# A convolution and LoRA layer on one core: gate mixing in eight tiles of the matmul array, conv weights by halves, and a new order of the first 620 steps

## The chip, the core and the metric

The kernel runs on one core of one Trainium2 chip. The metric is the device time of one execution in microseconds (us); the time shown is the median of several. A core has five engines that work side by side: TensorE (PE in the profile; PEld is its loading of weights), VectorE (DVE), ScalarE (ACT), GpSimd (POOL) and SyncE (SP), which here only issues DMAs. ACT issues DMAs too.

## The reference

The input `x` has shape (64, 64, 1024). A grouped 1-D convolution (4 groups, 9 taps) with a conditional bias goes in front of a linear layer with two LoRA terms; the result is added to `x`:

```python
out = lax.conv_general_dilated(x, weight, ..., feature_group_count=4)
y = out + einsum('nd,od->no', c, c_weight)[:, :, None] + bias[None, :, None]
...
base_out = matmul(y, kernel) + bias
A_eff = einsum('bn,nri->bri', gate, lora_A)
B_eff = einsum('bn,nor->bor', gate, lora_B)
delta = einsum('bor,btr->bto', B_eff, einsum('bri,bti->btr', A_eff, y))
delta = delta + einsum('or,btr->bto', lora_B_shared, einsum('ri,bti->btr', lora_A_shared, y))
x = x + base_out + delta
```

There are 8 gates of 16 entries; gate b mixes the 16 LoRAs for 8 samples. The shared LoRA is one for all.

## The kernel before

**Tiling.** The 64 samples are worked on as 16 pairs `p` of 4 samples each. For each pair and each of the four groups `g` the input is loaded (`xload`, 258 KB), split into a rounded high part and a rest (`xhi` on ACT, `xlo` on VectorE or GpSimd), and convolved by matmuls against a Toeplitz form of the weights, which is split in the same way (`th`, `tl`); three products high x high, low x high and high x low give the precision. Pairs 0 to 2 convolve directly (`conv`, 6 matmuls, line 318), later ones by a scheme with three half-size products, whose middle one (`convo`) uses the sum of the two weight blocks, and whose outer ones (`convd`) use differences of the input (`xdiff`, `xdhi`, `xdlo`, `xohi`, `xolo`; line 346). `evac` brings a convolution from PSUM to SBUF with its bias, `turned` transposes it on VectorE (line 387).

**The linear layer.** Pair 0 is multiplied plainly (`plain`, 3 matmuls, line 580), the other pairs by a Strassen-Winograd scheme of seven products on blocks of 512 x 512 (`prod`, 12 matmuls each, line 592), with block sums of the activations (`asum` on GpSimd) and of the weights (`wsum`), and splits `yhi`/`ylo` and `whi`/`wlo`. The weight pieces are loaded (`wload`), the shared LoRA's product is made by 16 matmuls (`fmm`, line 475, from `saload`, `sbload` and their splits) and added to them (`fadd`, line 479, VectorE). `keep`, `xsum`, `ysum`, `radd`, `yadd`, `total` combine the products with the residual (`rload`), and `store` writes 256 KB.

**The gated LoRA.** `lload w i` loads 16 tiles `ls` of 256 KB. `gload` and `gmask` build `gm`, the gates on a diagonal mask (lines 506 to 513). `mix w j` (line 528) multiplies: two float32 products of K 128, M 64, N 512 into the two halves of one PSUM tile. `mixout` (line 534, ACT) copies it over an `ls` tile, `mixput` (line 542) writes it in two DMAs of 128 KB to a DRAM tensor `eff`, and `aload` (line 550) and `bload` (line 556) read a gate's part back: 128 KB for A, three times 64 KB for each half of B. `lora p` (line 602) is 16 products of M 32 in four column tiles; `axlow`, `axsum`, `axhi`, `axlo` split its result, and `delta` (line 660) adds it to the accumulators.

**PSUM.** Five buffers of one bank each serve `fmm`, `mix`, `plain`, `prod` and the conditional bias (`cmul`), two serve the convolutions, one serves `lora`. A new user waits for the evacuation of an old one: `fmm` for a `fadd`, a convolution for its `evac` or `evmid`.

**Order.** One list, ORDER, of 1848 steps is written out in the code. Each step issues its instructions on its engines in this order, and no engine reorders. The last letter of a step chooses the engine: v VectorE, p GpSimd, a ACT. `xload`, `wload`, `lload`, `rload`, `mixput`, `aload`, `bload` issue on SP; `small`, `cwload`, `gload`, `ctload`, `store` on ACT. All DMAs share eight completion slots: each waits until the eighth before it has landed.

The start of the list, with `busy` (warming matmuls, line 701), `twload`, `thi`, `tlo`, `twsum` (weights of the convolution), and `cwide`, `cmul`, `csum` (conditional bias):

```python
small 1, warm, twload 1, busy 29, twload 0, cwload, gload, ctload, cwide, cmul, thi 2, small 0, thi 0, tlo 0 v,
xload 0 0, xhi 0 0, tlo 2 p, xload 0 1, xlo 0 0 v, conv 0 0, twsum v, xhi 0 1, xlo 0 1 v, conv 0 1, sbload 1,
```

Of the kernel before, what the change touches and what calls it, by code (L numbers as in the profile page):

```python
# [10 lines left out]
ALU = mybir.AluOpType  # L11
# [39 lines left out]
small 1, warm, twload 1, busy 29, twload 0, cwload, gload, ctload, cwide, cmul, thi 2, small 0, thi 0, tlo 0 v,  # L51
xload 0 0, xhi 0 0, tlo 2 p, xload 0 1, xlo 0 0 v, conv 0 0, twsum v, xhi 0 1, xlo 0 1 v, conv 0 1, sbload 1,
sbhi 1, csum, evac 0 0 v, turned 0 0, xload 0 2, xhi 0 2, xload 0 3, saload 0, sblo 1 p, xlo 0 2 p, evac 0 1 v,
turned 0 1, saload 1, gmask, xhi 0 3, conv 0 2, xlo 0 3 p, sahi 1, conv 0 3, sahi 0, salo 0 v, fmm 0 1,
sbload 0, sbhi 0, fmm 1 1, wload 1 0, evac 0 2 a, xload 1 0, sblo 0 v, fmm 1 0, salo 1 v, xload 1 1, xhi 1 0,
xhi 1 1, xlo 1 1 p, xlo 1 0 v, turned 0 2, yhi 0 0, ylo 0 0 p, wload 0 1, fadd 0 1, evac 0 3 a, fadd 1 0,
conv 1 0, whi 7 0, fmm 4 0, turned 0 3, xload 1 2, xhi 1 2, wlo 7 0 v, fmm 3 0, wload 1 1, conv 1 1, fadd 1 1,
wload 4 0, fmm 0 0, whi 0 1, wload 0 0, fadd 0 0, evac 1 0 a, plain 0 1 0, fadd 4 0, xlo 1 2 p, turned 1 0,
whi 0 0, wlo 0 1 p, fmm 2 1, fmm 2 0, yhi 0 7, evac 1 1 a, conv 1 2, fmm 5 0, wload 2 1, wload 2 0, fadd 2 0,
wlo 0 0 p, plain 0 0 0, xload 1 3, fadd 2 1, wload 5 0, xhi 1 3, fmm 4 1, xlo 1 3 p, plain 0 0 1, whi 0 2,  # L60
ylo 0 7 v, fadd 5 0, plain 0 3 0, whi 7 1, yhi 0 4, wload 3 0, fadd 3 0, whi 0 3, wload 5 1, fmm 3 1, conv 1 3,
turned 1 1, wlo 7 1 v, wload 3 1, xload 2 0, plain 0 1 1, fadd 3 1, whi 7 2, evac 1 2 v, wlo 7 2 p, wload 4 1,
wlo 0 3 p, wlo 0 2 v, lload 0 6, plain 0 2 0, whi 7 3, plain 0 3 1, fadd 4 1, wload 7 1, turned 1 2, whi 1 1,
plain 0 1 2, lload 0 7, xhi 2 0, plain 0 0 2, ylo 0 4 v, plain 0 3 2, xlo 2 0 v, plain 0 2 1, fmm 5 1,
evac 1 3 a, xload 3 0, wlo 7 3 v, plain 0 2 2, turned 1 3, whi 1 0, yhi 0 1, ylo 0 1 v, fadd 5 1, whi 6 1,
conv 2 0, wload 7 0, thi 1, xdiff 3 0 0 v, wload 6 0, evac 2 0 a, lload 1 5, wlo 1 0 p, fmm 7 0, fadd 7 0,
plain 0 2 3, plain 0 0 3, fmm 6 0, lload 0 2, plain 0 3 3, plain 0 1 3, fadd 6 0, lload 0 5, whi 6 0, asum 1 2,
yhi 1 2, lload 0 0, yhi 1 0, plain 0 0 4, plain 0 2 4, wsum 2 2 v, whi 2 2, lload 1 1, wlo 1 1 p, plain 0 0 5,
fmm 6 1, tlo 1 v, plain 0 2 5, rload 0 2, wlo 6 0 v, wsum 2 1 v, wsum 2 3 v, whi 1 2, wlo 1 2 v, plain 0 1 4,
whi 2 1, asum 1 3, whi 1 3, wlo 1 3 p, xload 2 2, wload 6 1, fadd 6 1, xload 2 1, whi 6 2, lload 0 1, xhi 2 2,  # L70
plain 0 3 4, lload 0 4, plain 0 2 6, lload 1 0, lload 0 3, wsum 2 0 v, fmm 7 1, plain 0 2 7, xload 2 3,
plain 0 0 6, fadd 7 1, whi 6 3, total 0 2, lload 1 6, mix 0 0, mixout 0 0 a, wlo 6 2 v, xhi 2 1, wlo 6 3 v,
wlo 6 1 v, wsum 3 2 v, xlo 2 2 v, mix 0 3, mixout 0 3 a, mix 0 2, mixout 0 2 a, wsum 3 0 v, wsum 5 0 v,
mixput 0 0, whi 2 3, mix 0 1, wsum 3 1 v, mix 1 0, mixput 0 3, mixout 0 1 a, xdiff 3 0 1 p, wsum 4 0 v,
conv 2 2, wlo 2 2 v, whi 2 0, wlo 2 0 v, ylo 1 2 v, plain 0 1 5, wsum 5 1 v, rload 0 0, wsum 5 2 v, wsum 4 2 v,
xlo 2 1 v, plain 0 0 7, mixput 0 1, ylo 1 0 p, mixput 0 2, wlo 2 1 v, prod 1 0, plain 0 1 6, wsum 3 3 v,
wsum 5 3 v, rload 0 1, plain 0 3 5, wsum 4 3 v, bihi, whi 3 2, keep 1 0, plain 0 1 7, lload 1 3, wsum 4 1 v,
plain 0 3 6, mixout 1 0 a, lload 1 7, mix 1 3, aload 0, whi 5 3, yhi 1 3, rload 0 3, lload 1 2, ylo 1 3 v,
mixout 1 3 a, total 0 1, lora 0, mix 1 1, turned 2 0, lora 1, whi 5 0, bilo, xohi 3 0, lload 1 4, mix 1 2,
whi 4 2, wlo 4 2 v, mixout 1 1 a, xolo 3 0 v, whi 3 0, wlo 3 0 v, wlo 3 2 v, yhi 1 1, ylo 1 1 v, mixout 1 2 a,  # L80
asum 1 5, total 0 0, whi 4 1, conv 2 1, axlow 1, axsum 1, xload 3 2, wlo 4 1 p, wlo 2 3 v, whi 4 0,
plain 0 3 7, axlow 0, axsum 0, mixput 1 0, mixput 1 3, wlo 4 0 v, xhi 2 3, xlo 2 3 v, wlo 5 3 v, axhi 1,
prod 1 1, biput 0, axlo 1, whi 3 3, asum 1 6, yhi 1 6, wlo 3 3 v, mixput 1 1, evac 2 1 a, turned 2 1, aload 1,
mixput 1 2, total 0 3, evac 2 2 v, turned 2 2, bload 0 0, whi 3 1, axhi 0, prod 1 2, keep 1 2, conv 2 3,
bhi 0 0, biput 1, yhi 2 0, evac 2 3 a, blo 0 0 v, axlo 0, yhi 1 4, bload 0 1, wlo 3 1 p, prod 1 3, ylo 2 0 v,
delta 0 0 1, total 0 0 1, bhi 0 1, blo 0 1 v, ylo 1 6 p, prod 1 6, whi 4 3, delta 0 3 1, wlo 4 3 v, store 0 0,
# [12 lines left out]
yadd 1 v, blo 1 0 v, xdhi 4 0, axlo 2, delta 2 0, yhi 2 6, evac 3 3, keep 2 2, xdlo 4 0 v, convo 4 0,
turned 3 3, convd 4 0, rload 2 0, evmid 4 0 a, total 1 3, total 2 0, ylo 3 0 v, lora 3, xdiff 4 1 0 v,  # L100
xdiff 4 1 1 p, asum 3 3, yhi 3 3, prod 3 0, convo 4 1, ylo 3 3 v, evac 4 0, turned 4 0, xdhi 4 1, xload 4 3,
xohi 4 3, xdlo 4 1 v, asum 3 2, xolo 4 3 v, yhi 3 2, ylo 2 6 v, xload 4 2, xdiff 4 2 0 p, store 1 2,
xdiff 4 2 1 p, xohi 4 2, prod 3 3, yhi 3 1, bload 1 1, evmid 4 1 a, delta 2 2, ylo 3 2 v, xolo 4 2 v, asum 3 5,
store 2 0, convd 4 1, xdhi 4 2, xsum 2, convo 4 2, evmid 4 2 a, evac 4 1, xdlo 4 2 v, rload 2 2, radd 2 2 p,
total 2 2, xdiff 4 3 0 v, xdiff 4 3 1 p, prod 2 6, turned 4 1, yhi 3 4, bhi 1 1, convd 4 2, evac 4 2, keep 3 0,
prod 3 2, ylo 3 1 v, rload 2 3, radd 2 3 v, ysum 2 v, convo 4 3, yadd 2 v, xdhi 4 3, xdlo 4 3 v, ylo 3 4 v,
aload 2, prod 3 1, convd 4 3, turned 4 2, blo 1 1 p, xload 5 0, yhi 3 5, xohi 5 0, keep 3 2, asum 3 6,
keep 3 3, xload 5 1, xohi 5 1, delta 2 3, prod 3 4, delta 2 1, xdiff 5 0 0 p, xdiff 5 0 1 v, axlow 3,
ylo 3 5 p, evmid 4 3 a, total 2 3, prod 3 5, store 2 3, xolo 5 0 p, rload 2 1, yhi 3 6, radd 2 1 p, rload 3 0,
axsum 3, evac 4 3, axhi 3, turned 4 3, yhi 4 0, axlo 3, delta 3 0, xload 5 2, xdhi 5 0, store 1 3, xdlo 5 0 v,  # L110
# [707 lines left out]
```

## Time and profile before

| what | value |
|---|---|
| median of 3 runs | 447.79 us (447.44 to 451.44) |
| the profiled execution's own time | 447.48 us |
| its span in the profile | 445.7 us |
| TensorE busy | 438.3 us, 98% |
| VectorE busy | 391.3 us, 88% |
| ACT busy | 251.2 us, 56% |
| GpSimd busy | 234.5 us, 53% |
| DMA | 67.05 MB, mean 150 GB/s |

Times in the profile count from the span's start. Busy time is the union of an engine's instructions; ends of matmuls are modelled, so one matmul's record overlaps the next one's, and what a matmul really takes is read from one start to the next. A row of a group has the line of the code, the engine, the operation, the tiles (out<-in), the count, and after the bar the busy time, the mean length in ns and the idle time before.

### The profile page before, as it was taken

The numbers are of one execution on the slowest core, as the hardware profiler recorded it, in microseconds if no ns is written. First come the engines' busy times: TensorE is split into PE (matmuls) and PEld (weight loads), VectorE is DVE, ScalarE is ACT, GpSimd is POOL, SyncE is SP. The second block draws the span as 40 slices with busy tenths as digits, with TensorE's granted clock in tenths as the row PEclk, the third lists the DMA queues.
The fourth block names the chain that finished last, engine by engine and source line by source line (L and its number), as shares of the span: only waits on it lengthen the run. The fifth ranks groups of instructions, "written<-read, shape, count | busy, mean of one in ns | idle before, by whom it ended". The sixth has DMA issues, their size and how long they took to land.

```text
span 445.7 us, 7717 instructions
## 1 busy us (share of the span) xinstructions
PE 438.3 (98%) x2557; PEld 358.7 (80%) x2557; DVE 391.3 (88%) x615; ACT 251.2 (56%) x639; POOL 234.5 (53%) x202
## 2 busy tenths in 40 slices
PE   8999999999999999999999999999999999999996
PEld 7677658888888888888878888888888888888884
DVE  5998979899899899889899899899798989887783
ACT  5877468556655566446555655646554745654440
POOL 3766024754747653555444445464656475467543
PEclk9999999999999999999999999999999999999999
DMA  8999582461625463534345453443536354262243
GB/s 229 300 280 308 147 251 66 142 186 49 186 82 158 136 190 110 170 120 136 97 139 147 151 182 91 119 142 90 175 98 186 95 169 151 72 222 90 91 150 118
DMA packets 52488, 67.05 MB, mean 150 GB/s; under 512 B 6112, under 2 KB 34016, under 8 KB 52448
## 3 DMA queue, kind: packets, MB, share of 16 engines
q1 hardware_dynamic: 42512, 49.83, 38.9%
q10 hardware_dynamic: 9936, 16.73, 10.2%
q8 instruction: 20, 0.33, 0.3%
q14 instruction: 20, 0.16, 0.1%
HBM read 47.65 MB, written 18.87 MB: 149 GB/s over the span
## 4 chain that ended last, share of the span: by engine, by line
PE 91%; DMA 4%; DVE 2%; issue 1%; SPq 0%; ACT 0%; ACTq 0%; DVEq 0%
PE mm_a L592 19%; PE mm_d L592 18%; PE mm_c L592 17%; PE mm_b L592 9%; PE cv L346 8%; PE cm L346 4%; PE axp L602 3%; PE cv L318 2%; DMA wr<-in_dram 2%; PE mx L528 2%; PE mm_a L580 1%; PE mm_c L580 1%; DMA ls<-in_dram 1%; DMA ctt<-in_dram 1%; PE mm_d L580 1%; PE mm_a L660 1%
## 5 line engine op out<-in xcount | busy, mean ns | idle before, releaser
L592 PE MATMUL mm_a<-wh,y 128*128 128x512 f32 x240 | 79.6, 392 | 0.0
L592 PE MATMUL mm_d<-wh,y 128*128 128x512 f32 x240 | 79.2, 391 | 0.0
L592 PE MATMUL mm_c<-wh,y 128*128 128x512 f32 x240 | 79.1, 391 | 0.0
L364 ACT ACTIVATE md<-cm,cadd 128x64 f32<-128x64 f32 x208 | 48.2, 315 | 44.8 <-PE cm L346 41.1
L326 POOL TENSOR_TENSOR xf<-xt 128x256 f32<-128x256 f32 x45 | 33.3, 747 | 49.4 <-DVE xd L270 39.4
L265 ACT CAST xd<-xf 128x512 fp32r<-128x512 f32 x52 | 32.5, 626 | 44.9 <-PE cv L346 20.7
L265 ACT CAST y<-s 128x512 fp32r<-128x512 f32 x60 | 37.2, 624 | 30.5 <-POOL s L412 15.3
L592 PEld LDWEIGHTS mm_a<-wh,y 128*128 128x128 f32 x240 | 45.1, 188 | 9.9 <-issue 0.4
L592 PEld LDWEIGHTS mm_d<-wh,y 128*128 128x128 f32 x240 | 45.1, 188 | 9.2 <-issue 0.2
L592 PEld LDWEIGHTS mm_c<-wh,y 128*128 128x128 f32 x240 | 45.1, 188 | 9.1 <-ACT c L636 0.2
L387 DVE STREAM_TRANSPOSE z<-v 128x512 f32<-128x512 f32 x64 | 45.4, 709 | 3.2 <-PE axp L602 1.9
L592 PE MATMUL mm_a<-wl,y 128*128 128x512 f32 x120 | 46.9, 391 | 0.0
L592 PE MATMUL mm_c<-wl,y 128*128 128x512 f32 x120 | 46.8, 390 | 0.0
L592 PE MATMUL mm_d<-wl,y 128*128 128x512 f32 x120 | 46.8, 390 | 0.0
L346 PE MATMUL cv<-xd,th 128*128 128x256 f32 x208 | 45.7, 282 | 0.4 <-DVE xd L270 0.4
L378 DVE TENSOR_TENSOR v<-cv,md 128x512 f32<-128x512 f32 x52 | 35.7, 686 | 7.7 <-PE cv L346 2.5
L270 DVE TENSOR_TENSOR xd<-xf,xd 128x512 fp32r<-128x512 f32 x41 | 34.5, 842 | 7.6 <-ACT xd L265 7.4
L270 DVE TENSOR_TENSOR y<-s,y 128x512 fp32r<-128x512 f32 x49 | 38.2, 782 | 3.0 <-ACT y L265 2.7
L592 PE MATMUL mm_b<-wh,y 128*128 128x512 f32 x120 | 39.6, 391 | 0.0
L346 PEld LDWEIGHTS cv<-xd,th 128*128 128x128 f32 x208 | 35.5, 188 | 2.4 <-DVE xd L270 0.6
L265 ACT CAST y<-z 128x512 fp32r<-128x512 f32 x49 | 30.6, 625 | 11.8 <-DVE c L641 4.5
L326 DVE TENSOR_TENSOR xf<-xt 128x256 f32<-128x256 f32 x59 | 33.7, 587 | 0.2
(132 smaller groups left out, 1008.2 us busy)
## 6 DMA issues: line engine op xcount, KB each, us to landing
xt<-in_dram SPq DMA_DIRECT2D x64, 258.0 KB, 3.2
r<-in_dram SPq DMA_DIRECT2D x64, 256.0 KB, 3.5
out_dram<-r ACTq DMA_DIRECT2D x63, 256.0 KB, 2.6
ls<-in_dram SPq DMA_DIRECT2D x16, 256.0 KB, 4.6
br<-eff SPq DMA_DIRECT2D x48, 64.0 KB, 2.8
wr<-in_dram SPq DMA_DIRECT2D x16, 176.0 KB, 4.2
eff<-ls SPq DMA_DIRECT2D x16, 128.0 KB, 2.7
wr<-in_dram SPq DMA_DIRECT2D x16, 80.0 KB, 3.9
```

Source lines behind the costliest of these rows:

```text
L265: nc.scalar.copy(dst, src)
L270: engs[eng].tensor_tensor(dst, src, f32(hi), ALU.subtract)
L318: nc.tensor.matmul(ps, a[:, 2 * kt, g, :], b[:, :, kt:kt + P], start=(n == 0), stop=(n == 5))
L326: engs[eng].tensor_tensor(xdf[p, g][:, e], m, odd(p, g), ALU.subtract)
L346: nc.tensor.matmul(ps, a[:, w, g, :], b, start=(n == 0), stop=(n == 2))
L364: nc.scalar.activation(t[:, n], cpm[p, g][:, n], ACTF.Identity, bias=c[:, n:n + 1])
L378: nc.vector.tensor_tensor(v.rearrange("p n (i e) -> p e n i", e=2), cps.pop((p, g)), mid.pop((p, g)).unsqueeze(1).to_broadcast([P, 2, 4, H ...
L387: nc.vector.transpose(z[:, :, :, :, gg, :], vs.pop((p, g)).rearrange("p m j -> p (m j)"))
L528: nc.tensor.matmul(mps[w, j][n * e:n * e + n], gm.rearrange("p b i -> p (b i)"), lraw[w, 2 * j + e], start=True, stop=True)
L580: nc.tensor.matmul(acc[p, BLOCKS[b]], m[:, kk, :], n, start=(k == 0 and q == 0), stop=(k == 7 and q == 2))
L592: nc.tensor.matmul(ps, a[:, k, :], b[bb, k], start=s, stop=(k == HK - 1 and q == 2), skip_group_check=not first)
L602: nc.tensor.matmul(axp[q * R:q * R + R, p % 2, :], a[:, k, :], zs[p, hf][:, k, :], start=k < 2, stop=k >= 6)
```

## The change

It has three parts.

**The gates in eight tiles.** `mix` takes its eight products from four `ls` tiles and from both halves of the partitions: K 64, M 32, N 512, four column places and two row halves, the two halves into two PSUM tiles. There are four mixes instead of eight; `mixout` and `mixput` take one PSUM tile each, eight times as before. `gm` has half the columns. `eff` is laid out by column place, gate, and then the rest, and `aload` and `bload` read it accordingly.

**Conv weights by halves of the groups.** `twload h`, `thi h`, `tlo h` handle groups 2h and 2h + 1 with both weight blocks, where each handled one block of all four groups; the sum of the blocks is made and split in two halves (`twsum h`, `thm h`, `tlm h`).

**A new order of the first 620 steps.** It holds the same steps (but for the mixes and conv weights), in another order, with some v and p exchanged; steps 621 to 1848 are the same on every engine. Its start:

```diff
-small 1, warm, twload 1, busy 29, twload 0, cwload, gload, ctload, cwide, cmul, thi 2, small 0, thi 0, tlo 0 v,
-xload 0 0, xhi 0 0, tlo 2 p, xload 0 1, xlo 0 0 v, conv 0 0, twsum v, xhi 0 1, xlo 0 1 v, conv 0 1, sbload 1,
...
+warm, twload 0, xload 0 1, sbload 1, busy 28, busy 4, cwload, gload, gmask, ctload, thi 0, xload 0 0, sbload 0,
+twload 1, twsum 1 p, xhi 0 1, tlo 0 v, twsum 0 v, xlo 0 1 v, sbhi 1, sblo 1 v, cwide, cmul, small 0, saload 0,
+xhi 0 0, xlo 0 0 v, conv 0 0, sbhi 0, sblo 0 v, thi 1, tlo 1 p, wload 1 0, wload 0 1, conv 0 1, csum, sahi 0,
...
+    HI = GC // 2
+    eff = [dram.tile([4, NB, 2, 2, 2, HI, AW], F32, tag=f"eff{w}", name=f"eff{w}") for w in range(2)]
...
-        n = NB * GC
-        for e in range(2):
-            nc.tensor.matmul(mps[w, j][n * e:n * e + n], gm.rearrange("p b i -> p (b i)"), lraw[w, 2 * j + e],
-                             start=True, stop=True)
+        for r in range(2):
+            mps[w, j, r] = pl.tile([P, 2 * AW], F32, tag=tag, name=f"mx{w}_{j}_{r}")
+        n, m = NB * HI, P // 2
+        for e in range(4):
+            for r in range(2):
+                nc.tensor.matmul(mps[w, j, r][n * e:n * e + n], gm[m * r:m * r + m].rearrange("p b i -> p (b i)"),
+                                 lraw[w, 2 * e + j][m * r:m * r + m], start=True, stop=True)
...
-    def mixput(w, j):
-        n = NB * GC
-        for e in range(2):
-            dst = eff[w].rearrange("c p a -> p c a")[:, 4 * j + 2 * e:4 * j + 2 * e + 2, :]
-            nc.sync.dma_start(dst, mev[w, j][n * e:n * e + n].rearrange("p (c a) -> p c a", c=2))
+    def mixput(w, j, r):
+        for c in range(2):
+            dst = eff[w][:, :, j, c, r].rearrange("e b i a -> (e b) i a")
+            nc.sync.dma_start(dst, mev[w, j, r][:, c * AW:c * AW + AW])
...
-        nc.sync.dma_start(ar[b].rearrange("p k r -> p (k r)"), eff[0][:, GC * b:GC * b + GC, :])
+        nc.sync.dma_start(ar[b].rearrange("p k r -> p (k r)"), eff[0][:, b].rearrange("e j c r i a -> e (j c r i a)"))
...
-        src = eff[1][:, GC * b:GC * b + GC, :].rearrange("c (e q) a -> c e (q a)", e=2)[:, :, HN * h:HN * h + HN]
+        src = eff[1][:, b].rearrange("e j c r i a -> e (j c r) (i a)")[:, :, HN * h:HN * h + HN]
...
+    def thi(h):
+        hi_of(th[:, 0:3:2, 2 * h:2 * h + 2], twr[h])
+    def tlo(h, eng="v"):
+        lo_of(tl[:, 0:3:2, 2 * h:2 * h + 2], twr[h], th[:, 0:3:2, 2 * h:2 * h + 2], eng)
...
+    def twsum(h, eng="v"):
+        tws[h] = slot("r", f"tws{h}", (P, 2, P))
+        engs[eng].tensor_tensor(tws[h], twr[h][:, 0], twr[h][:, 1], ALU.add)
```

The places on TensorE that the prediction speaks of, in the new order: `fmm 4 0` and `fmm 2 1` stand behind `fmm 0 1`, then `conv 0 3, fadd 0 0, conv 0 2, whi 0 0, ..., plain 0 1 0, wlo 7 2 v, wlo 0 0 v, ..., plain 0 0 0`. Around the mixes:

```diff
+xhi 2 2, xlo 2 2 v, lload 0 3, mix 0 1, lload 1 4, mixout 0 1 1 a, lload 1 2, plain 0 1 6, rload 0 3,
...
+lload 1 7, lload 1 3, whi 5 3, lload 1 5, total 0 1, wlo 5 3 v, whi 3 3, wlo 3 3 v, aload 0, mix 1 1,
...
+evac 3 3, turned 3 3, lora 3, xdhi 4 0, xdlo 4 0 p, evmid 4 0 a, asum 2 5, yhi 2 5, rload 2 0, yadd 1 v,
```

## The prediction

> **What bounds the kernel now.** I read the page's busy row first, then the stretches (busy time by stage), then who waited for whom, then instructions in order of time.
>
> ```profile
> PE 438.3 (98%) x2557; PEld 358.7 (80%) x2557; DVE 391.3 (88%) x615; ACT 251.2 (56%) x639; POOL 234.5 (53%) x202
> ```
>
> TensorE is busy nearly the whole span, with VectorE second. The stretches, whose columns are PE, PEld, DVE, ACT, POOL, granted clock, DMA share and GB/s, show how this differs by stage (140.40 is where the last TensorE step of the reordered part ends):
>
> ```profile
> 0.00:20.00 20.00, 17.54 (x80) 13.74 (x81) 14.94 (x23) 12.87 (x27) 9.73 (x14) 1.00 0.92 257
> 20.00:40.00 20.00, 20.00 (x87) 15.89 (x86) 18.99 (x31) 15.47 (x36) 13.16 (x10) 1.00 0.96 293
> ...
> 60.00:80.00 20.00, 19.65 (x130) 14.66 (x121) 17.81 (x31) 17.44 (x42) 6.85 (x5) 1.00 0.43 123
> ...
> 140.40:440.70 300.30, 299.87 (x1816) 251.07 (x1815) 265.25 (x422) 162.84 (x431) 160.76 (x137) 1.00 0.44 134
> ```
>
> From 140.4 us on TensorE has no hole (299.87 of 300.30) and nothing changes there; so the time changes by what happens to the end of the head. In the head VectorE is about as full as TensorE (18.99 of 20), so a saving on TensorE counts only where VectorE keeps up. The clock is full everywhere.
>
> The waits of TensorE before 141 us are few and early, but a modelled end hides more: a matmul lasts 0.39 in the record and is followed after 0.227.
>
> ```profile
> PE cv L318 <- POOL xsl L270: 0.6, 1, 0.6
> PE cv L318 <- DVE xsl L270: 0.4, 1, 0.4
> PE mx L528 <- DMA ls<-in_dram: 0.4, 1, 0.4
> ```
>
> Prices of TensorE, from start to start in the timeline: 12 matmuls of a prod 2.72, a plain step 0.68, a conv 6 x 0.236, convd 6 x 0.118, lora 1.01, a shared-LoRA product (fmm) 0.234. With these the head holds 132.4 us of TensorE work, beginning at 1.18; it ends at 140.4, so 6.8 us are lost in it: some 3.2 before the first plain step at 19.9, 1.6 around the mixes, the rest in crumbs.
>
> **Part 1, the mixes.** Five mixes in a row, then three single ones:
>
> ```profile
> 44.10 4.74 PE L528 MATMUL mx<-ls,gm 128*64 128x512 f32 x20
> ...
> 57.19 2.24 PE L528 MATMUL mx<-ls,gm 128*64 128x512 f32 x4
> ...
> 60.80 1.08 PE L528 MATMUL mx<-ls,gm 128*64 128x512 f32 x4 [0.35 <-DMA ls<-in_dram]
> ```
>
> A mix is two products of two records each, and takes 4.67/5 = 0.93 alone; the eight with their waits take 4.67 + 2.17 + 1.4 + 1.0 = 9.2. The one at 57.19 waited in its middle for the second load. The new mix is eight products (K 64, M 32) in eight tiles, four times instead of eight. lora is the nearest row: 16 products on four tiles, 32 records, in 1.01, where the tiles start together. So a new mix is 0.43 x 2 passes plus starting = 1.0, and four are 4.0: 5.2 less with the old waits, 3.6 without them. Row tiling is not in the trace; if row tiles did not overlap at all, a mix would take 2.0 and the gain were nothing. I take 4.0, as the column tiles of lora overlap fully. ACT evacuates eight tiles of 0.59 before and after; SP issues 16 writes and 16 loads before and after. A mix now waits for four loads and two PSUM buffers where it waited for two and one.
>
> The mixed weights lie otherwise in DRAM: the outermost dimension that aload and bload read shrinks from 16 to 4. By the Trainium skill, "DMA: Bandwidth & Descriptors", section "Why a DMA increments its semaphore by 16 and not by 1", a copy runs on the largest number of engines up to 16 that divides both sides' outer dimensions: four now. The row is `ar<-eff`, 128 KB, 3.3 to landing. At 293 GB/s over 16 engines (busy in the second stretch) 128 KB on four engines take 1.7 and not 0.4, so 4.6 by the rule, 3.3 by the row (estimates). aload 0 can leave some 7 after mix 0 1 (evacuations 1.2, four writes 2.6, landing 2.7); between mix 0 1 and lora 0 stand 10.3 of TensorE work and 1.0 for mix 1 1. By the row lora 0 does not wait, by the rule about 0.3 and, if SP is late, 1 to 2. I take nothing and keep 2 for the range; in the tail the loads leave about 10 before their lora.
>
> **Part 2, the conv weights by halves.** The sum of taps and its split become two half-size instructions each: VectorE +0.0 to 0.2, ACT +0.1. twsum 1, tlo 1 and the two salo move to GpSimd at some 1.29 each, where they lie before its first asum. The first conv can begin on 256 KB of weights and not 512 (the first load landed at 3.84, the second at 4.59). That is not used: xload 0 0 is now the fourth load (second load of x), and the mask of the gates now stands ahead of everything on VectorE, waiting for gg. Before, gg was issued at 1.67 and took 3.7; issued second on ACT at 1.19 it lands at 4.9. Then VectorE has 0.1 + 0.68 + 0.36 + 0.69 + 0.68 before cwide: 7.4 to 7.6. cwide takes 1.5 in the trace because it stood behind a GpSimd subtraction (4.71 to 6.00) and ended 0.28 after it; alone I take 0.3 to 0.9. So cmul starts at about 8.0 (before 6.58) and conv 0 0 at 8.9 (before 7.47): 1.4 of TensorE lost, of which 3 more warming matmuls fill 0.36 only. SP's and ACT's loads share eight slots, and a load waits for the eighth before it (SP waited 1.4 us for the tiny bias load); with bias and fs later, five large loads leave at once, and what the new order needs by each step asks for at most 255 KB per us (2.57 MB by 13 us), before 262. So I cost loads at nothing; this cover is thin only until 20 us, and a load late there delays fadd, then plain, one for one.
>
> **Part 3, the order of 620 steps.** All other steps are the same in kind and number; some 50 change between VectorE and GpSimd, in both directions, with 58 GpSimd steps before and after. What matters is which engine is ahead where. I counted, in the new order, what stands ahead of lora 3, the last place of the head where TensorE needs late VectorE work (turned 3 3):
>
> - TensorE: 101.7 us of work before, 92.0 after (two prods fewer, 5.4; mixes 3.6; convd 0.7; a delta 0.2). Behind it 30.7 before, 37.1 after.
> - VectorE: 147 instructions, 96.2 us at prices alone (0.685; 0.415 for 256 columns; 0.71 a transpose) before; 145 and 93.3 after. GpSimd: 41 steps before, 36 after.
>
> So VectorE is asked for 93.3 us by a point that TensorE could reach at 1.18 + 92.0 + its early losses (some 4.5: 1.4 of part 2, then fmm 4 0 waiting for a PSUM buffer that fadd 0 1 frees, 1 to 1.7, fmm 2 1 0.45, plain 0 0 0 waiting for its wlo 0.8 to 1.1) = 97.7. In the old order VectorE reached it at 109.3, from 4.78 on: 96.3 busy by the stretches and 8.2 idle or between instructions.
>
> Prices alone are not what VectorE pays. A VectorE instruction with both inputs in SBUF does not run beside a GpSimd one:
>
> ```profile
> 121.78 1.29 POOL L412 TENSOR_TENSOR s<-z,s 128x512 f32<-128x512 f32 x1
> 122.01 1.61 DVE L270 TENSOR_TENSOR y<-z,y 128x512 fp32r<-128x512 f32 x1
> ```
>
> The subtraction ends 0.55 after GpSimd's 123.07, and takes 0.68 where GpSimd is idle. The groups give the mean price of this:
>
> ```profile
> L270 DVE TENSOR_TENSOR xd<-xf,xd 128x512 fp32r<-128x512 f32 x41 | 34.5, 842 | 7.6 <-ACT xd L265 7.4
> L270 DVE TENSOR_TENSOR y<-s,y 128x512 fp32r<-128x512 f32 x49 | 38.2, 782 | 3.0 <-ACT y L265 2.7
> L326 DVE TENSOR_TENSOR xf<-xt 128x256 f32<-128x256 f32 x59 | 33.7, 587 | 0.2
> ```
>
> 842, 782 and 587 against 685, 680 and 415 alone: with the other such groups about 45 us over some 198 GpSimd instructions, 0.23 each. The Trainium skill, "SBUF — State Buffer", section "Who interferes with whom", says that the later one is blocked until the first has finished; if each of 36 GpSimd steps caught one VectorE instruction in its middle, that is 36 x 0.65 = 23 us and lora 3 would come at 120. The measured 0.23 stands for the mixture that these orders have, so I take it: 36 x 0.23 = 8.3, 1.1 less than 41 of them.
>
> VectorE in the new order: start 4.9 to 5.1; busy 96.3 x 93.3/96.2 - 1 = 92.4; idle between 0 (97.4) and the old 8.2 (105.6). Half of the old idle was waiting for TensorE (1.9 for the LoRA product, 1.4 for deltas, 1.2 for fmm), and there TensorE is now early; so I take 4.3: turned 3 3 at 101.7. Then 37.1 of TensorE work follow with VectorE ahead: head end 101.7 + 37.1 + 0.2 = 139.0, against 140.4.
>
> **The sum.** The profiled execution took 447.48 (span 445.7 and 1.8 around it). -1.4 gives 446.1; the median of the runs shown is 447.79, 0.3 above, so **446.4**. TensorE's own bill falls by 3.3 (132.4 to 129.1: mixes -3.6, warming +0.4); 2 of it is eaten by VectorE.
>
> **Rivals.** (a) VectorE is not the limit: it idles little, lora 3 comes at TensorE's 97.7, head end 135.0 to 135.4, time 442.4. For it: ACT and GpSimd have room (15.5 and 13.2 of 20). Against it: VectorE would need 93 us of work in 93. Chance 0.2. (b) Slower, one mechanism at one place: VectorE blocked by GpSimd up to turned 3 3. Each us that this step comes later than 103.1 is lost outright; at 0.45 a GpSimd step and not 0.23, with the old idle of 8.2, it comes at 113 and the time is 458; from 107.6 on it is slower by 1%. For it: the new order puts 22.1 us of VectorE prices in the first 20 of TensorE's work (before 18.3). Chance 0.15. (c) Row tiles don't overlap, so the change does not do what it says: mixes cost 8.0 and TensorE's own way to lora 3 is 101.7, just what VectorE needs anyway; 446.5 to 448.5. Chance 0.1, inside my own case's range.
>
> **How the numbers follow.** My case with (c) 0.65: VectorE's idle between 1 and 8 and its start 0.5 either way put the head's end between 135.7 and 143.4, so 443.1 to 450.8. The range over all cases, 442.4 (no idle) to 452.5 (head end +4.7: old idle, start late, 0.06 more for each GpSimd step), leaves out the rest of (b) and a little of (a). This kernel's measurement can tell about 1%, 4.5 us. Faster by over 1% is (a): 0.2; slower by over 1% is (b): 0.15; within: 0.65.
>
> **What would show it.** Mix records of 1.0 (tiles starting together) or 2.0; cmul near 8.0; turned 3 3 and lora 3 near 101.7 (97.7: rival a; beyond 107: rival b), and TensorE's head end 37 us behind it; VectorE's subtractions ending 0.55 after a GpSimd one. I am wrong if TensorE waits for a load or for ACT between 20 and 100 us, or if the part after the head, which I hold at 300.3, changes by over 1 us because of what the head leaves behind.

## The result, and the profile after

| | before | after |
|---|---|---|
| median | 448.24 us (447.44 to 451.44, 4 runs) | 459.65 us (458.00 to 460.19, 4 runs) |
| ratio, 95% interval | | 1.0243 (1.0203 to 1.0284): slower |
| profiled execution, span | 447.48, 445.7 | 458.00, 456.0 |
| delta 3 3 begins, the end of the reordered head | 140.42 | 145.36 |
| from there to the end | 305.3 | 310.6 |

The forecast was 446.4 us with a range to 452.5. The profiled execution is 10.5 us longer: 4.9 in the head, which was to be 1.4 shorter, and 5.3 behind it, where no instruction was changed. The page's busy row:

```profile
PE 444.0 (97%) x2592; PEld 360.4 (79%) x2592; DVE 394.0 (86%) x620; ACT 249.1 (55%) x628; POOL 237.0 (52%) x202
```

TensorE is still the busy one. The stretches of the kernel after (PE, PEld, DVE, ACT, POOL, granted clock, DMA share, GB/s), cut at the end of turned 3 3 and at the start of lora 4:

```profile
5.00:105.59 100.59, 94.50 (x549) 71.54 (x548) 92.35 (x148) 67.60 (x158) 48.98 (x37) 1.00 0.70 212
105.59:145.92 40.33, 40.28 (x212) 33.27 (x212) 34.01 (x50) 17.02 (x38) 29.42 (x24) 0.96 0.29 96
145.92:456.00 310.08, 305.45 (x1817) 251.73 (x1816) 266.71 (x421) 162.55 (x430) 157.59 (x135) 1.00 0.42 132
```

and the last one of the kernel before, also from lora 4 on:

```profile
140.97:445.70 304.73, 300.27 (x1817) 251.35 (x1816) 265.43 (x424) 162.48 (x431) 160.72 (x136) 1.00 0.44 135
```

The same 1817 records of TensorE take 5.2 us more of busy time at the same clock. So it is not a wait. The timeline shows what it is. Three matmuls of a prod before (start, length):

```profile
149.21 0.39 PE L592 MATMUL mm_d<-wh,y 128*128 128x512 f32 x1
149.44 0.39 PE L592 MATMUL mm_d<-wl,y 128*128 128x512 f32 x1
149.67 0.62 PE L592 MATMUL mm_d<-wh,y 128*128 128x512 f32 x2
```

and after:

```profile
147.39 0.39 PE L596 MATMUL mm_a<-wh,y 128*128 128x512 f32 x1
147.62 0.40 PE L596 MATMUL mm_a<-wl,y 128*128 128x512 f32 x1
147.86 0.63 PE L596 MATMUL mm_a<-wh,y 128*128 128x512 f32 x2
```

One follows the other after 0.23 and 0.23 before, 0.23 and 0.24 after. Over all plain and prod matmuls the median time from the start of one to the start of the next, called the spacing below, is 227 ns before and 234 after (means of those under 300: 228.4 and 234.1), from the first microsecond of plain work to the last. 5.7 ns by some 1350 such matmuls is 7.7 us; some 1000 of them, 5.7 us, lie from lora 4 on. The other TensorE forms kept their spacing (256 columns 118 in both, conv 236 and 235).

In the head TensorE waited here (first column the sum, last the longest):

```profile
PE axp L606 <- DVE z L388: 2.1, 1, 2.1
...
PE pf L476 <- DVE wr L480: 1.2, 1, 1.2
PE mm_d L596 <- POOL y L271: 0.8, 1, 0.8
PE mm_d L584 <- DVE wl L271: 0.7, 1, 0.7
PE axp L606 <- DMA ar<-eff: 0.6, 1, 0.6
```

The first is lora 3, which has the transposed tile of turned 3 3 as its input. In order of time:

```profile
104.87 0.71 DVE L388 STREAM_TRANSPOSE z<-v 128x512 f32<-128x512 f32 x1
...
105.64 1.41 PEld L606 LDWEIGHTS axp<-z,ar 128*32 128x32 f32 x30 [2.34 <-DVE z L388]
105.64 1.87 PE L606 MATMUL axp<-z,ar 128*32 128x128 f32 x30 [2.07 <-DVE z L388]
...
107.44 0.58 PE L347 MATMUL cm<-xo,th 128*128 128x256 f32 x1
```

The matmuls stand 2.07 us (the loads of their weights 2.34); then the records come at half rate, and lora 3 takes 1.8 us instead of 1.0. The granted clock is 0.72 in 104 to 108 us and 0.85 in 108 to 112, from one stretch of 3.41 us at 0.50 that begins at 105.8; over 100 to 120 it is 0.91, and it is 1.00 there in the kernel before.

### The profile page after: what moved, and what is told of

The parts are those of the page before. It is cut to its first block, busy times and chain, and to the rows that moved or that the text cites. A ratio compares the mean times of both kernels' runs of the same rounds, so it can differ in the third digit from the quotient of the medians.

```text
span 456.0 us, 7762 instructions
## 1 busy us (share of the span) xinstructions
PE 444.0 (97%) x2592; PEld 360.4 (79%) x2592; DVE 394.0 (86%) x620; ACT 249.1 (55%) x628; POOL 237.0 (52%) x202
## 4 chain that ended last, share of the span: by engine, by line
PE 78%; DVE 9%; DMA 6%; issue 3%; SPq 1%; ACT 1%; POOL 1%; DVEq 0%; ACTq 0%; POOLq 0%
PE mm_a L596 16%; PE mm_c L596 15%; PE mm_d L596 15%; PE mm_b L596 8%; PE cv L347 7%; PE cm L347 4%; PE axp L606 4%; PE cv L319 2%; DVE r L653 1%; PE mm_c L584 1%; PE mm_b L584 1%; PE mm_d L584 1%; DMA r<-in_dram 1%; DMA out_dram<-r 1%; PE mm_a L584 1%
## 5 line engine op out<-in xcount | busy, mean ns | idle before, releaser
L596 PE MATMUL mm_d<-wh,y 128*128 128x512 f32 x240 | 80.7, 397 | 0.8 <-POOL y L271 0.8
L596 PE MATMUL mm_a<-wh,y 128*128 128x512 f32 x240 | 80.8, 398 | 0.0
L596 PE MATMUL mm_c<-wh,y 128*128 128x512 f32 x240 | 80.5, 396 | 0.0
L365 ACT ACTIVATE md<-cm,cadd 128x64 f32<-128x64 f32 x196 | 45.6, 316 | 36.3 <-PE cm L347 32.3
L271 POOL TENSOR_TENSOR xd<-xf,xd 128x512 fp32r<-128x512 f32 x15 | 21.1, 1407 | 38.9 <-ACT xd L266 38.8
L413 POOL TENSOR_TENSOR s<-z,z 128x512 f32<-128x512 f32 x15 | 22.4, 1495 | 27.4 <-DVE y L271 13.3
```

Of the source, the lines that this page charges most:

```text
L271: engs[eng].tensor_tensor(dst, src, f32(hi), ALU.subtract)
L365: nc.scalar.activation(t[:, n], cpm[p, g][:, n], ACTF.Identity, bias=c[:, n:n + 1])
L413: engs[eng].tensor_tensor(t, m, n, op)
L596: nc.tensor.matmul(ps, a[:, k, :], b[bb, k], start=s, stop=(k == HK - 1 and q == 2), skip_group_check=not first)
```

## The experiments

The theories at the outset: **A**, the new order lets the compiler's allocation put the weight tiles at other on-chip addresses, and TensorE streams them more slowly from there; **B**, the order itself makes the spacing. A had a reason: the regions of on-chip memory follow the order in which the kernel first uses each kind of buffer, and the new order changes that. Addresses below are those of the compiled programs, within a partition. The kernel shows where the shift comes from: in the new order the first weight tile (`sbload 1`) stands ahead of the first `xhi`, so the regions of `xd` (4128 bytes) and `xo` (two tiles of 2064, each rounded up to 2080) now lie between the weights and y. Together they are 8288 bytes, 96 over a multiple of 256; all else between is a multiple of 256. Each set of runs has runs of the kernel before beside it on the same chip.

**The weights on a multiple of 64 bytes.** In the kernel before wh and wl lay on multiples of 64 bytes, after 32 past one.

```diff
     def piece(name, shape=(P, HN), dtype=F32):
+        pad("pad0")   # one 32-byte tile ahead of the weights, another behind them
```

> The changed kernel with one thing moved: a 32-byte tile is set ahead of the weight tiles and another behind them, so that the address of every wh, wl, sa, sb and ls tile within a partition goes from 32 past a multiple of 64 bytes to a multiple of 64 bytes, as it is in the kernel before; every other tile keeps its place modulo 64. Order, instructions and arithmetic are those of the changed kernel. Theory A (the changed order lets the weight tiles' region begin at another address, and TensorE reads 512-column operands there more slowly): the matmuls of plain and prod start 227 ns apart again instead of 234, some 1300 of them by 6 ns each is about 8 us, and the time is 450 to 452 us, with the part behind the head back at about 305 us. Theory B (the spacing comes from the order of the steps or from something else of the change): 459 to 460 us, spacing 234 ns.

456.43 us (ratio 1.0172, 1.0139 to 1.0206), spacing 232. Between both: the place of wh alone is not it.

**The kernel before, weights moved by 32 bytes**, the same pads in the other kernel.

> The kernel before with the weight tiles shifted the other way: 32 bytes ahead of them, 32 behind, so that they lie 32 past a multiple of 64 and every other tile keeps its place modulo 64. Nothing else differs. Theory A (address of the weight tiles): the spacing goes from 227 to 234 ns and the time to about 456 us (448.2 plus 1300 by 6 ns; less, down to 454, where the head is held by VectorE). Theory B (the order): no change, 448 us.

454.08 us (1.0121, 1.0088 to 1.0154), spacing 232 to 233. The order is the old one and the spacing is slow, so B is out as the only cause.

**gm at its old size.**

```diff
-    gm = const.tile([P, NB, HI], F32, name="gm")
+    gm = const.tile([P, 2 * NB, HI], F32, name="gm")[:, 0:NB]
```

> The changed kernel with the mask tile gm allocated at its old size of 256 bytes in a partition (half of it unused), so that everything allocated behind it moves by 128 bytes to where a 256-byte mask would put it. It tells a second form of the address theory from the first. If the shrunken mask is what moved the weights into the slow position (theory A2), the spacing falls to 227 ns and the time to about 451 us. If only the place modulo 64 counts (theory A), nothing changes: 234 ns and 458 to 460 us.

460.09 us (1.0248, 1.0198 to 1.0298), 234: a shift of everything by 128 bytes does nothing.

**The kernel before, all streamed operands on multiples of 64.**

```diff
+    const.tile([P, 8], F32, name="padc")           # bst on 64
...
+        pad("pad0")                                # in piece, the weights on 64
...
-            xss[p, g] = [work.tile([P, 4, JB], F32R, tag="xo", ...
+            xss[p, g] = [work.tile([P, 528], F32R, tag="xo", ...)[:, 0:4 * JB] ...
```

> The kernel before with every operand that TensorE streams set on a multiple of 64 bytes: a 32-byte tile ahead of bst, one ahead of the weights, and the buffers of the xo tag rounded up to 2112 bytes; bst, axt, xd and the second xo buffer were 32 past one. In the trace of before some 360 of 1290 plain and prod matmuls start 230 to 238 ns apart, most of them just behind delta, convd or fmm. Theory A (the place of the streamed operand, whose slower reads also delay what follows them): most of those fall to 227, delta from 237 to 227, and the time falls by 1 to 3 us, to 445 to 447. Theory B: no change, 448.

449.26 us (1.0019, 1.0002 to 1.0036), 227, and the slow ones are not fewer: 413 of 1338 at 230 ns or over, where the kernel before has 321. The expected gain did not come, and theory A in this form fell. But in this run wh and y had both moved by 128 bytes, and in the first wh had moved against y. That gave theory **C**: what counts is the distance between the streamed wh or wl and the stationary y, whose next block is loaded while the former streams.

**The changed kernel in the old layout.**

```diff
+    for tag, n in (("r", 4), ("s", 2), ("xt", 2), ("xo", 2), ("xd", 1), ("w", 57)):
+        work.tile([P, 8], F32, tag=tag, name=f"claim_{tag}", bufs=n)
```

> The changed kernel, its order and its instructions, with the working memory laid out as in the kernel before: the buffers' regions are claimed in the order in which the kernel before first used them, and gm keeps its old size, so that the region of the weights (w) and that of the left operands (y) begin at the same addresses as before, a whole multiple of 2048 bytes apart. Theory C (what counts is how far the streamed wh or wl lies from the stationary y, not the place of wh alone, since the runs with both moved by the same 128 bytes kept 227 ns and the run with wh on a multiple of 64 but 128 bytes off y did not): spacing 227 to 229 ns, some 1320 by 5.6 ns or 7.4 us less than the changed kernel, 451 to 453 us, the part behind the head back at about 305 us, and what is left against the kernel before, 3 to 4 us, all in the head. Theory B (the spacing belongs to the order): 458 to 460 us, 234 ns.

454.41 us (1.0104, 1.0068 to 1.0139), spacing 227, and 306.2 us from lora 4 on instead of 310.1. The timeline of a prod there:

```profile
148.04 0.39 PE L596 MATMUL mm_a<-wh,y 128*128 128x512 f32 x1
148.27 0.39 PE L596 MATMUL mm_a<-wl,y 128*128 128x512 f32 x1
148.49 0.62 PE L596 MATMUL mm_a<-wh,y 128*128 128x512 f32 x2
```

So the layout is worth 5.2 us of the loss by the two medians (459.65 to 454.41), and 6.2 with each set held against the kernel before beside it (11.4 and 5.2 us slower). In the traces the part from lora 4 on is 3.9 shorter, and lora 4 itself came no earlier (146.6, and 145.9 in the kernel after); where the rest of the gain lies was not found.

**Everything up by 64; y up by 128, 512, 256, 64 bytes against the weights**, all in the kernel before:

```diff
+    const.tile([P, 16], F32, name="padc")          # everything from bst on, 64 bytes
...
+        pad("pad1", 128)                           # ahead of v, z and y; also 512, 256, 64
         v = vs[p, g] = work.tile(
```

> The kernel before with everything from bst on moved up by 64 bytes, weights and left operands alike. Their distance stays a multiple of 2048 bytes; their place modulo 128 changes from 64 to 0. Theory C (distance): no change, 227 ns, 448 us. Theory D (place modulo 128, which the runs so far do not exclude): 232 ns and 453 to 455 us.

> The kernel before with 128 bytes set between the weights and the left operands y: wh and wl stay where they were, y (with v, z and what is behind them) goes up by 128 bytes; every place modulo 128 stays. Theory C (distance): 232 to 233 ns, some 1320 by 4 ns, 453 to 454 us. Theory D (place modulo 128): no change, 227 ns and 448 us.

> As the run with 128 bytes between weights and left operands, but with 512 bytes. If the distance counts modulo 512 or less (one k-block of y is 512 bytes, so distances of a multiple of 512 occur within a tile anyway): no change, 227 ns and 448 us. If it has to be a multiple of 2048: 232 to 234 ns and 453 to 455 us.

> The kernel before with 256 bytes between the weights and the left operands y, to find the period in which their distance counts (512 bytes between them changed nothing, 128 made 232 ns of 227). If the period is 256: no change, 227 ns. If it is 512: 231 to 235 ns and 453 to 455 us.

> The kernel before with 64 bytes between the weights and the left operands y, to complete the row of distances (0, 256 and 512 gave 227 ns; 32, 96 and 128 gave 232 to 234). If every distance but a multiple of 256 is slow: 231 to 234 ns and 453 to 455 us. If a multiple of 64 is enough except 128: 227 ns.

All kernels in one table, by the distance y minus wh modulo 256 bytes; the spacing is the median (mean of those under 300):

| distance | kernel | spacing ns | from lora 4 to the end | median us |
|---|---|---|---|---|
| 0 | before | 227 (228.4) | 304.7 | 448.2 to 449.2 |
| 0 | before, all up 64 | 227 (228.2) | 304.7 | 448.97 |
| 0 | before, y up 512 | 227 (228.3) | 304.8 | 449.14 |
| 0 | before, y up 256 | 227 (228.3) | 305.0 | 451.71, one run |
| 0 | before, all on 64 | 227 (228.7) | 305.2 | 449.26 |
| 0 | after, old layout | 227 (228.4) | 306.2 | 454.41 |
| 32 | before, w up 32 | 232 (233.0) | 308.9 | 454.08 |
| 64 | before, y up 64 | 233 (233.3) | 309.1 | 454.62, one run |
| 96 | after | 234 (234.1) | 310.1 | 459.65 |
| 96 | after, gm at its old size | 234 (234.0) | 310.9 | 460.09 |
| 128 | before, y up 128 | 232 (232.7) | 308.3 | 453.88 |
| 128 | after, w on 64 | 232 (232.5) | 308.5 | 456.43 |

The order of the steps does not matter for the spacing, nor does any place by itself; a distance that is a multiple of 256 bytes is fast, the four others that occurred are slow. Theory C holds in all twelve, and in the seven runs below, all at distance 0 with 227. Each pad moved v, z, xf and q along with y, so no run separates y from these by itself. But wh, wl and y are all that these matmuls read, and the work of the other engines makes no difference: in the kernel after, the mean spacing is 234.1 where VectorE, ACT and GpSimd all work (204 matmuls), 234.6 where ACT and GpSimd are idle (144) and 233.6 where VectorE is idle and the other two work (27); before it is 228.6, 227.6 and 228.5. Why the distance counts is not shown. The single runs show the spacing, and their times little: with nothing changed in the order, lora 4 came at 140.5 to 144.9 us, mostly by the first 20 us, so a head of one profile is good to some us only.

**The rest of the loss, some 5 us in the old layout.** First lora 3, moved behind prod 2 4:

```diff
-evac 3 3, turned 3 3, lora 3, xdhi 4 0, ..., prod 2 4,
+evac 3 3, turned 3 3, xdhi 4 0, ..., prod 2 4, lora 3,
```

> The changed kernel in the layout of before (as in the run before this one, 454.4 us), with one step moved: lora 3 issued behind prod 2 4 instead of ahead of convo 4 1, so that TensorE works on prod 2 4 (12 matmuls, 2.7 us) while VectorE finishes evac 3 3 and turned 3 3. In the changed kernel's trace lora 3 waited 2.3 us for turned 3 3, and its records then ran at half rate with the granted clock at 0.91 in 100 to 120 us, about 1.5 us more. Theory P (only the place of this step was wrong for VectorE's real pace): 2.5 to 4 us less, 450.5 to 452 us. Theory V (VectorE is the limit of the head; the wait only moves to the next step that needs it, such as convd 4 0 or prod 3 0): 453.5 to 454.5 us.

452.46 us (1.0098, 1.0076 to 1.0120): no wait at lora 3, clock 1.00, but TensorE now stands 1.4 us at convd 4 0 (L349, waiting for VectorE's evac). Its ratio overlaps that of the base, so the same wait was removed from the other side, beside a repeat of the base:

```diff
-convd 3 3, axlo 2, ..., radd 1 3 v, keep 2 3, evac 3 3, turned 3 3, lora 3,
+convd 3 3, evac 3 3, turned 3 3, axlo 2, ..., radd 1 3 v, keep 2 3, lora 3,
```

> The changed kernel in the layout of before (454.4 us), lora 3 in its place, with evac 3 3 and turned 3 3 set on VectorE directly behind convd 3 3, ahead of axlo 2, xdiff 4 0 0, blo 1 0, xolo 4 1 and radd 1 3 (some 2.7 us at the prices of the trace). Theory P (the wait of lora 3 for turned 3 3, with the slow records behind it, is a loss by itself): turned 3 3 comes 1.5 to 2.5 us earlier, lora 3 hardly waits, its records take 1 us and not 1.9, and the time falls by 2 to 3.5 us, to 451 to 452.5. Theory V (VectorE is the limit up to here, and what is postponed is late in turn at convd 4 0 or prod 3 0): 453.5 to 454.5 us, with waits of the same sum just behind lora 3.

> The changed kernel in the layout of before once more, unchanged, beside the run with turned 3 3 first on the same chip, since the runs that it is compared with differ by less than two chips do: 454 to 455 us.

452.92 us (1.0085, 1.0067 to 1.0102) against 454.64 (1.0120, 1.0096 to 1.0145) for the base: about 1.7 us, between the two theories. The intervals overlap a little (1.0096 to 1.0102), so the gain is likely and not certain. TensorE's waits from 70 us on in the run with turned 3 3 first:

```profile
PE mm_c L598 <- DVE r L672: 1.0, 1, 1.0
...
PE mm_b L598 <- DVE r L672: 0.3, 1, 0.3
```

The base waits 2.1 at lora 3; here 1.3 have come back at the products behind it, which need PSUM that VectorE frees. The clock of 100 to 120 us is 1.00 (base: 0.91), though this trace has a slow stretch at 9.3 us, as the base has one at 16.6. Read from these waits, 0.8 of the 2.1 was the place of one step, with the slow clock behind it, and the rest is VectorE's pace.

**gmask later on VectorE:**

```diff
-cwload, gload, gmask, ctload, ..., turned 0 0, saload 1,
+cwload, gload, ctload, ..., turned 0 0, saload 1, gmask,
```

> The run with lora 3 behind prod 2 4 (452.5 us), with gmask issued behind saload 1, as in the kernel before, instead of as VectorE's second step: there its reduction waits for gg, and cwide, cmul and conv 0 0 behind it came 1.4 to 1.5 us later than in the kernel before. If that late start is carried through the head (theory S), the idle matmuls end 1.4 us earlier and the time falls by 1 to 1.5 us, to about 451 us. If the head is held by something later (theory V: VectorE's work up to turned 3 3, or the fmm steps that wait for their fadd), cmul is earlier and the time stays at 452 to 453 us.

454.12 us (1.0114, 1.0085 to 1.0142), and cmul began at 8.19, no earlier than in the run that it is compared with (7.96). What VectorE waits for there:

```profile
DVE tl L273 <- ACT th L268: 3.7, 1, 3.7
```

Behind gmask stands tlo 0, which waits for ACT's thi 0 and holds cwide as long. Neither theory: the start is late for another reason.

**The mixes alone, in the old order and layout:**

```diff
-mix 0 0, mixout 0 0 a, ..., mix 0 3, mixout 0 3 a, mix 0 2, mixout 0 2 a, ..., mix 0 1, ..., mixout 0 1 a,
+mix 0 0, mixout 0 0 0 a, mixout 0 0 1 a, ..., mix 0 1, ..., mixout 0 1 0 a, mixout 0 1 1 a,
...
-lora 0, mix 1 1, turned 2 0, lora 1, ..., mix 1 2,
+lora 0, mix 1 1, turned 2 0, lora 1, ..., mix 1 0,
```

> The kernel before with the mixes in eight tiles alone: its order, its loading of the convolution weights and its memory layout (gm padded to its old size) stay; eight mixes become four, two issued where the third and fourth of the first pair of operands stood, two where the last two of the second stood, with copies and stores to match. In the traces the mixes took 8.9 us of TensorE before and 4.75 after. Theory T (TensorE is the limit of the head): 4 us less, 444.5 to 445.5 us. Theory V (VectorE is: turned 3 3 ended 1.2 us ahead of lora 3 in the kernel before, so a TensorE that is 4 us earlier waits there for some 3 us): 1 to 2 us less, 447 to 448 us, with a wait at lora 3.

457.07 us (1.0201, 1.0174 to 1.0228): slower than either theory had it. TensorE's longest waits:

```profile
PE dl L664 <- DVE axt L627: 4.0, 1, 4.0
PE axp L606 <- DMA ar<-eff: 3.7, 1, 3.7
```

TensorE came to lora 0 at 56.7 instead of 59.4, but the mixed rows came no earlier: they wait for the last lload, the copies, the writes and the read back. Behind each of the two waits the clock stood at 0.50 for 3.41 us (0.91 over the stretch of 20 us). The mixes themselves took 6.4 us here and not 4.75, since one of two in a row waits 0.7 for a buffer and another runs at the slow clock. With the waiting steps put behind other work:

```diff
-plain 0 3 6, ..., lora 0, mix 1 1, turned 2 0, lora 1, ..., conv 2 1, ..., plain 0 3 7,
+plain 0 3 6, conv 2 1, plain 0 3 7, ..., mix 1 1, lora 0, turned 2 0, lora 1,
...
-delta 0 0 1, total 0 0 1, bhi 0 1, blo 0 1 v, ylo 1 6 p, prod 1 6,
+ylo 1 6 p, prod 1 6, delta 0 0 1, total 0 0 1, bhi 0 1, blo 0 1 v,
...
-lora 3, ..., prod 3 0,
+..., prod 3 0, lora 3,
```

> The kernel before with the mixes in eight tiles, as in the run of the mixes alone (457.1 us), and with the steps that waited there put behind other work of TensorE: conv 2 1 and plain 0 3 7 (2.1 us) and mix 1 1 ahead of lora 0, turned 2 0 with it, prod 1 6 (2.7 us) ahead of delta 0 0 1, lora 3 behind prod 3 0. In the run of the mixes alone TensorE came to lora 0 at 56.7 us and waited 3.9 us for the gathered rows of ar, then 4.1 us at delta 0 0 1 for bst, each followed by a stretch with the granted clock at 0.91. Theory T (TensorE is the limit once nothing waits for those chains of copies and transfers, so the 4.1 us that the mixes free are saved): 444.5 to 446 us. Theory V (VectorE sets the pace of the head too; the mixes free TensorE of 4 us that it then waits): 447.5 to 449.5 us. If the chains of transfers are later than this cover: 450 us or more, with the wait still at lora 0 or at delta 0 0 1.

454.53 us (1.0126, 1.0102 to 1.0149): the third case. lora 0 no longer waits, delta 0 0 1 and its neighbour wait 0.7 and 2.3 (the longer one for bst), and in the profiled execution (456.41 us) the clock stood at 0.50 for 10.2 us in all. This is the chain that the new order had to make room for; no run here made the mixes pay.

**aload 4 behind the rloads:**

```diff
-bload 3 0, aload 4, asum 6 2, rload 5 3, ..., rload 5 1,
+bload 3 0, asum 6 2, rload 5 3, ..., rload 5 1, aload 4,
```

> The run with lora 3 behind prod 2 4 (452.5 us), with aload 4 issued behind rload 5 3 and rload 5 1 instead of ahead of them. In every kernel with the new layout of eff, and in none with the old one, VectorE's radd 5 3 waits 3.2 us for r instead of 1.6 and TensorE stands 0.7 us at the next convo. Theory L (the aload's read in the new layout occupies the queue longer and delays the load behind it): that stall of 0.7 us is gone, and r waits under 2 us. Otherwise (the delay has another cause): it stays. The time alone, 451.5 to 453, will hardly tell; the trace does.

451.75 us (1.0068, 1.0038 to 1.0098). VectorE's wait for r, in the kernel before, in the run with lora 3 moved, and in this one:

```profile
DVE r L649 <- DMA r<-in_dram: 1.6, 1, 1.6
```

```profile
DVE r L655 <- DMA r<-in_dram: 3.2, 1, 3.2
```

```profile
DVE r L655 <- DMA r<-in_dram: 2.5, 1, 2.5
```

TensorE's 0.7 us behind it shrank to 0.2. Partly as theory L had it: the read of the mixed rows delays the load behind it, but the wait did not fall to its old length. The three reads of bload 3 0, in the new layout too, still stand ahead of the rloads; no run moved them. The time from lora 4 on was 305.7 against 306.3.

## Why the prediction was wrong

Its own sum, for the profiled execution, was 446.1; it took 458.0. Of the 11.9 us, 6.4 are in the head (139.0 forecast, 145.4 measured), 5.3 behind it, 0.2 around.

- **The mixes: right.** A mix of 1.0 was forecast:

```profile
46.98 1.09 PE L533 MATMUL mx<-ls,gm 64*32 64x512 f32 x16
47.99 0.50 PE L584 MATMUL mm_d<-wh,y 128*128 128x512 f32 x1
```

  1.01 from the first tile to the next step. From first tile to next step the four took 4.75 us, 0.7 of it the wait of lora 0 behind the last; the eight before took 8.86, and one stood 0.4 for its load besides. So 4.1 less (forecast 3.6 to 5.2). Rival (c) is out. It is the only gain, and the head has eaten it.
- **The read of the mixed rows: half seen.** The wait of lora 0 was 0.6; the prediction's row put it at nothing, the rule of engines for a copy in the Trainium skill ("DMA: Bandwidth & Descriptors", section "Why a DMA increments its semaphore by 16 and not by 1") at 0.3. The packets of the reads agree with the rule: from gate 2 on, the 128 packets of an aload were spread over 0.8 to 1.6 us before, with 15 to 20 under way at the busiest moment, and over 1.6 to 3.4 us after, with never more than 6; aload 4 took 0.8 before and 3.0 after. What I left out is that the load queued behind such a read is late too: r was waited for 1.6 longer, where the rule makes the read 1.3 longer (the prediction's 1.7 against 0.4, an estimate).
- **Conv weights: the size right, the reason wrong.** cmul at 8.10 and conv 0 0 at 9.01 (forecast 8.0 and 8.9), but not by gmask, as the run with gmask late shows: tlo 0 would hold cwide anyway.
- **TensorE's early losses: about right.** From start to start the fmm steps lost 2.2 us (forecast 1.5 to 2.2), the first plains some 1.2 (forecast 0.8 to 1.1).
- **VectorE up to turned 3 3: the term that failed in the head.** From 5.00 to 105.59 VectorE was busy 92.35 us; the forecast was 92.4. That it fits so well is luck. In the kernel before, turned 3 3 ended at 108.22 and not, as the prediction has it, at 109.3:

```profile
4.78:108.22 103.44, 101.71 (x535) 76.26 (x535) 95.25 (x149) 68.18 (x158) 51.71 (x43) 1.00 0.69 202
```

  From these 95.25 us of busy time its own working makes 91.4 (an estimate), so 1.0 more was spent than it would have said: the 1.1 that fewer GpSimd steps were to save did not come. Still VectorE's busy time fell by 2.9, so rival (b), VectorE blocked more than before, is not what happened; that (b) also named 458 us is chance, for it had turned 3 3 at 113. Rival (a) is out as well, since lora 3 waited for VectorE. The step that failed is "so I take 4.3" for VectorE's idle time: it was 8.2 (100.59 - 92.35), as before. I argued that half of the old idle was waiting for TensorE, which would now be early. Those waits were, before,

```profile
DVE z L387 <- PE axp L602: 1.9, 1, 1.9
DVE r L666 <- PE dl L660: 1.4, 2, 1.0
DVE wr L479 <- PE pf L475: 1.2, 2, 0.9
```

  and they shrank indeed, to the 1.1 in the third line below; waits for ACT's halves of the splits stand in their place:

```profile
DVE wl L271 <- ACT wh L266: 2.4, 3, 1.5
DVE y L271 <- ACT y L266: 1.1, 1, 1.1
DVE r L670 <- PE mm_c L584: 1.1, 1, 1.1
DVE bst L271 <- ACT bst L266: 0.8, 1, 0.8
```

  The two longest single waits, 1.5 for wl and 1.1 for y, come from TensorE after all, by way of ACT. On ACT a `mixout` stands ahead of the split and waits for its mix; the split behind it is late, and VectorE waits for that:

```profile
54.14 0.59 ACT L539 COPY ls<-mx 128x512 f32<-128x512 f32 x1 [2.28 <-PE mx L533]
54.62 0.62 ACT L266 CAST y<-s 128x512 fp32r<-128x512 f32 x1
55.28 0.69 DVE L271 TENSOR_TENSOR y<-s,y 128x512 fp32r<-128x512 f32 x1 [1.13 <-ACT y L266]
...
61.74 0.59 ACT L539 COPY ls<-mx 128x512 f32<-128x512 f32 x1 [2.57 <-PE mx L533]
62.22 0.62 ACT L266 CAST wh<-wr 128x512 fp32r<-128x512 f32 x1
62.87 0.69 DVE L271 TENSOR_TENSOR wl<-wr,wh 128x512 fp32r<-128x512 f32 x1 [1.51 <-ACT wh L266]
```

  So 2.6 of the idle time hangs on the copies of two mixes. This is read from the trace; no run moved the copies.

  In all, the idle time made turned 3 3 3.9 us late. Behind it 37.3 were forecast and 39.8 came. Of the 2.5, the clock explains at most 1.7 (28% of 4 us and 15% of the next 4; 0.8 of it in lora 3 alone), the spacing some 0.7 (about 130 matmuls by 5.7 ns).
- **"From 140.4 us on ... nothing changes there": the step that failed behind the head.** The prediction named it as what would make it wrong. No instruction changed and no stall of that size came; each streamed matmul took 5 to 6 ns longer, because the order of first use had moved the weights against y. In the old layout the part from lora 4 on is 306.2 to 306.7 and not 310.1; before it was 304.7. Of the 1.5 to 2 left, 0.6 is aload 4. Another 0.4 to 0.5 is lost at one convd, some 230 us behind lora 4, where TensorE waits for VectorE's evac in the traces of the old layout; why VectorE is late there was not followed.

In measured medians: 5.2 to 6.2 us of the loss are the layout; in the old layout the changed kernel is 5.2 to 5.6 us slower than the kernel before beside it, and of that about 1.7 is likely the wait at lora 3 with its slow clock, 1.5 to 2 lies behind the head (with the aload), and the remainder is the late start, the waits of fmm and plain and VectorE's idle time, less the mixes' 4.1. These last were read from traces and not separated by runs; nor was the new order, or the loading of the conv weights by halves, run by itself. No version here beats the kernel before.

## What to carry to other kernels

A new order, or a new tile, can move every address behind it: before comparing two orders, lay the buffers out alike, and compare the start-to-start time of an unchanged matmul in an unchanged stage first; a difference there explains microseconds that no wait shows. A saving on one engine is worth nothing where the chain of copies and transfers that it feeds ends as late as before, and a stall can cost a second time by the clock. An idle time taken from an old order is not halved because one of its reasons goes: say which other wait ends next, and follow it through the engines between, since a copy that waits holds up all that stands behind it.

## What the runs showed of the hardware

- Spacing of 512-column matmuls with 128 new stationary columns each: 227 ns where the stationary tile lies a multiple of 256 bytes from the streamed one (13 traces), 232 to 234 ns at distances of 32, 64, 96 and 128 over such a multiple (6 traces). The Trainium skill, "TensorE: Matmul & The Clock Gate", section "Step-by-step: what each phase is for", says that loading the next tile's weights doesn't steal read bandwidth from the running matmul. Here the place of the one relative to the other changed the pace by 2 to 3%; the measurement decides, whatever the way in which the two meet.
- Even at distance 0 some of these matmuls are slow: in the kernel before 321 of 1338 are at 230 ns or over, 307 of them among the first eight behind another kind of matmul (delta, convd, fmm and so on). Setting those operands on multiples of 64 bytes did not make them fewer; the cause is open.
- The clock after a wait of TensorE: where it falls, but for the end of the kernel, it stands at 0.50 for 3.41 us (once for 6.83) and is 1.00 again. The length of the wait alone does not decide. Lora 3's wait of 2.1 us was followed by such a stretch in three traces (the kernel after and twice its old layout) and by none in two (weights on 64, gm at its old size). The waits of 3.7 and 4.0 (the mixes alone) both were; waits of 1.7 to 1.8 at an fmm were in two traces of five, of 1.5 at an early conv in one of six, of 1.4 at convd 4 0 in none of three. The same page, section "🎯 Why this matters for your kernels", asks for no gaps over about 3 us; here shorter ones were enough in some traces. What else decides is not shown.
